# An attention kernel whose instruction order moves from hand-woven streams to a list scheduler

## The chip, the core and the metric

The kernel runs on one core of a Trainium2 chip. A core has five engines that run side by side, each on its own queue of instructions: TensorE (PE, matmuls and transposes into the PSUM banks), VectorE (DVE), ScalarE (ACT), GpSimd (POOL) and SyncE (SP, which here issues nearly all DMAs). [...] The metric is the device time of one execution in microseconds (us).

## The reference

Inputs are `x` (2 batches of 2048 rows, 640 wide) and a context of 128 tokens (384 wide) per batch, of which 124 are text and the last 4 feed an adapter. All is float32, 8 heads of 80. Cut to what matters:

```python
query = x @ Wq
hs = mha(query, text @ Wk, text @ Wv)              # text attention: 2048 queries, 124 keys
ca_q1 = einsum('btc,th->bch', ca, Wq_ca)           # (384, 640) from the 4 tokens
ca_q1 = ca_q1[:, indices]                          # 2048 rows, only 384 different ones
ca_hs1 = mha(ca_q1, x, x)                          # 384 queries over 2048 rows of x
ca_hs2 = mha(ca_hs1 @ Wq, ca @ Wk_ca, ca @ Wv_ca)  # over the 4 tokens
out = (hs + ca_hs2) @ Wout + b_out + x
```

So two things are computed for each batch: text attention, which is most of the work, and the adapter, a long chain whose result is a table `o2` of 384 rows that is added to the output rows by index.

## The kernel before

*Adapter.* `x` comes in blocks of 512 rows (4 per batch). `x_load` (L766) issues eight DMAs per block into one staging tile `xi`, and `x_turn` (L785) makes five 32-by-32 block transposes on VectorE into `xt`. `yz_block` (L800) multiplies a block by small prepared weights (`pyz`) and makes two operands, `yz` and `zop` (ScalarE copy, VectorE shuffle `zs`, ScalarE cast, VectorE subtraction). `maxima` (L843) goes over a batch in 24 steps: four matmuls (`s1`) fill one tile of four PSUM banks, VectorE takes the maximum of 2048 columns (`mx`). There is one such tile, so a step's matmuls wait for the maximum of the step before. `less_maxima` (L862) turns the maxima into an operand `cop`. `contraction` (L882) has 32 steps: four matmuls (`s2`) into the same tile, an exponential on ScalarE (`ea`), four matmuls that add it up with `y_sb` (`acc`). A short chain then gives `p2`, and `o2` is written to memory.

*Text.* `queries` (L991) makes the 25 matmuls `pq` of a block. A unit `m` is two tiles of 128 rows, 16 units in all. `scores` (L1026): ten matmuls `sc` per tile into two banks, maxima `m` and differences `p` on VectorE, exponential on ScalarE. `divided` (L1065): sums and reciprocals `r` on VectorE, product on POOL. `turned_out` and `turned` (L1089, L1075): a block transpose `eb`, written to memory as `kept` and read back as `pT`, which completes the transposition. `values` (L1114): 16 matmuls `ph`, copied out as `hsT`, then 20 output matmuls `po`, each half tile added on VectorE to the rows `xo` of `x` that `residual` (L1099) has loaded. If `o2` is already in memory, its rows are added by an indirect DMA on POOL (`add_second`, L1165) and the rows go out; otherwise they go to memory as `early`, and `completed` (L1173) fetches and finishes them later.

*What sets the order.* TensorE's instructions and SP's DMAs are pinned to program order. On VectorE a few instructions have order dependencies by hand (`VectorBehind`, L49); the rest of VectorE, ScalarE and POOL is ordered by the framework. Program order is woven from streams: `weave` (L1229) draws one step of the adapter, and then a `Mix` (L136) of `Fill`s (`own`, `text`, `later`) is run for as many microseconds of TensorE time as that step's gap says; TensorE's time is counted in `TensorInOrder` (L21). A fill is a fixed sequence of parts, and it stops at a part whose conditions are not met. `rows_stages` (L1284) holds the conditions of a block: its five transposes may come only when 18 or 24 us of TensorE work have passed since the load:

```python
stage(
    (("again" if again else "x") if k == 4 else ("turned", k), b, sb), x_turn(k),
    lambda k=k: Mix.hurry or pe.us > coming[0] + after + 0.6 * k,
)
```

PSUM has eight banks: four for the adapter's tile, three that text and the rest turn over in order (`mm_tile`, L263), and one that `acc` and some others use. When the adapter is done, its four go to text.

Of the kernel before, what the change touches and what calls it, by code (L numbers as in the profile page):

```python
# [14 lines left out]
P = 128  # L15
HEADS = 8
T = 4
WITHIN = "within"


class TensorInOrder:  # L21

    def __init__(self, tc):
        self.tc, self.us = tc, 0.0

    def matmul(self, out, lhsT, rhs, **kw):
        ins = self.tc.nc.tensor.matmul(out, lhsT, rhs, **kw)  # L29
        self.tc.keep_in_program_order(ins)  # L30
        n = 1
        for size in rhs.shape[1:]:
            n *= size
        if lhsT.dtype == F32R:
            self.us += (n / 2.4 + 215) / 4e3
        elif min(lhsT.shape[0], lhsT.shape[1]) <= 32:
            self.us += (n / 1.2 + 97) / 2e3
        elif min(lhsT.shape[0], lhsT.shape[1]) <= 64:
            self.us += (n / 1.2 + 54) / 1e3
        else:  # L40
            self.us += 2 * max(n / 1.2, 109) / 1e3

    def transpose(self, out, in_, ident):
        ins = self.tc.nc.tensor.transpose(out, in_, ident)
        self.tc.keep_in_program_order(ins)
        self.us += 0.109


class VectorBehind:  # L49

    def __init__(self, tc):
        self.tc, self.last, self.bound = tc, None, None

    def __getattr__(self, name):
        def call(*args, **kw):
            self.last = getattr(self.tc.nc.vector, name)(*args, **kw).ins  # L58
            if self.bound is not None:
                self.behind(self.last, self.bound)  # L60
            return self.last

        return call

    def behind(self, ins, other):
        kind = mybir.DependencyInfo(mybir.DependencyClass.NoSync, mybir.DependencyReason.DATA)
        self.tc.add_manual_dep(ins, other.name, kind, reason="order on VectorE")

    def close(self):
        self.bound = self.last  # L70


class Fill:


    def __init__(self, done, *parts):
        self.done, self.parts, self.open, self.us = done, list(parts), False, 0.0

    def add(self, *parts):
        self.parts += parts  # L80

    def blocked(self):

        return not self.parts or any(
            not w() if callable(w) else w not in self.done
            for w in getattr(self.parts[0], "needs", ())
        )

    def step(self, pe):

        if self.blocked():
            return False
        before = pe.us
        at = next(self.parts[0], self)
        self.us += pe.us - before
        self.open = at is WITHIN
        if at is self:
            self.parts.pop(0)
        return True


class Stage:


    def __init__(self, done, what, gen, *needs):
        self.done, self.what, self.gen, self.needs = done, what, gen, needs

    def __iter__(self):
        return self

    def __next__(self):
        self.needs = ()
        try:
            return next(self.gen)
        except StopIteration:
            self.done.add(self.what)
            raise


class Slots:  # L120


    def __init__(self, done, pool, number):
        self.done, self.pool = done, pool
        self.users = [set() for _ in range(number)]

    def free(self, n):
        return lambda: sum(u <= self.done for u in self.users) >= n

    def tile(self, shape, name, users):  # L130
        at = next(i for i, u in enumerate(self.users) if u <= self.done)
        self.users[at] = set(users)
        return self.pool.tile(shape, F32, tag=f"slot{at}", name=name)


class Mix:  # L136

    hurry = False  # L140

    def __init__(self, pe, *fills):
        self.pe, self.fills, self.at = pe, [[f, w, f.us] for f, w in fills], None

    def step(self):
        if self.at is not None and self.at.open:
            return self.at.step(self.pe)
        for f, w, us in sorted(self.fills, key=lambda x: (x[0].us - x[2]) / x[1]):
            if f.step(self.pe):
                self.at = f  # L150
                return True
        return False

    def run(self, us=None):

        while us is None or us > 0:
            before = self.pe.us
            if not self.step():
                return 0.0
            if us is not None:  # L160
                us -= self.pe.us - before
        return us

    def until(self, done, what):
        while what not in done:
            for f, _, _ in self.fills:
                if any(getattr(p, "what", None) == what for p in f.parts):
                    while self.at is not None and self.at is not f and self.at.open:
                        self.at.step(self.pe)
                    self.at = f  # L170
                    if not f.step(self.pe) and what not in done and not self.step():
                        Mix.hurry = True
                        assert f.step(self.pe), what
                        Mix.hurry = False
                    break
            else:
                assert what in done, what
# [3 lines left out]
def kernel(  # L181
# [14 lines left out]

    nc = tc.nc
    pe = TensorInOrder(tc)
    dve = VectorBehind(tc)
# [17 lines left out]
    MAX = 4 * T  # L241


    const = ctx.enter_context(tc.tile_pool(name="const", bufs=1))
    xrow = ctx.enter_context(tc.tile_pool(name="xrow", bufs=4))
    xqp = ctx.enter_context(tc.tile_pool(name="xqp", bufs=1))
    hbm = ctx.enter_context(tc.tile_pool(name="hbm", bufs=2, space=bass.MemoryType.DRAM))
    done = set()
    slots = Slots(done, xqp, NSB + 1)
    ps_m = ctx.enter_context(tc.tile_pool(name="ps_m", bufs=3, space=bass.MemoryType.PSUM))  # L250
    ps_a = ctx.enter_context(tc.tile_pool(name="ps_a", bufs=1, space=bass.MemoryType.PSUM))

    def dma(out, in_):

        tc.keep_in_program_order(nc.sync.dma_start(out, in_))

    matmul = pe.matmul
    transpose = pe.transpose

    ps_turns = [ps_m]  # L260
    ps_turn = [0]

    def mm_tile(name, pool=None):  # L263
        if pool is None:
            pool = ps_turns[ps_turn[0] % len(ps_turns)]
            ps_turn[0] += 1
        return pool.tile([P, 512], F32, tag="mm", name=name)

    on = ["A"]
    turn = [0]  # L270

    def evacuate(dst, src):

        turn[0] += 1
        if on[0][turn[0] % len(on[0])] == "A":
            nc.scalar.copy(dst, src)  # L276
        else:
            dve.tensor_copy(dst, src)

# [4 lines left out]
    def band(t, pattern, width, base=0):  # L284

        nc.gpsimd.memset(t, 1.0)
        nc.gpsimd.affine_select(
            out=t, in_=t, compare_op=ALU.is_ge, fill=0.0,
            base=base, pattern=pattern, channel_multiplier=1,
        )  # L290
        nc.gpsimd.affine_select(
            out=t, in_=t, compare_op=ALU.is_ge, fill=0.0,
            base=width - 1 - base, pattern=[[-a, n] for a, n in pattern], channel_multiplier=-1,
        )
# [6 lines left out]

# [5 lines left out]
    dve.tensor_reduce(ones, ones4, AX.X, ALU.add)  # L307

    VH = 2 * R
    VR = D - VH  # L310
# [9 lines left out]

# [3 lines left out]


# [11 lines left out]
    N2 = 3 * G + 2 * B * T  # L337
    w2_sb = const.tile([N2 + 1, H], F32, name="w2_sb")
    p2pad = const.tile([P, NCC, P], F32, name="p2pad")


    cap = ctx.enter_context(tc.tile_pool(name="cap", bufs=1))
    small = ctx.enter_context(tc.tile_pool(name="small", bufs=3))
# [3 lines left out]


    ctx_sb = sp.tile([NTOK, B, CAD], F32, name="ctx_sb")
    dma(ctx_sb, enc.rearrange("b t c -> t b c"))  # L350
    wqca_sb = sp.tile([T, H], F32, name="wqca_sb")
    dma(wqca_sb, Wq_ca)

    def by_chunk(t):

        g = t.rearrange("p (c d) -> p c d", c=4)
        return g[:, :, :P], g[:, :, P:]

    def load_x(b, st, name):
        t = xrow.tile([P, H], F32, tag="x", name=f"{name}_{b}_{st}")  # L360
        dma(t, x[b, st * P : (st + 1) * P, :])
        return t

    def block_rows(name):

        return xrow.tile([P, 4 * H], F32, tag="xz", name=name, bufs=1)
# [7 lines left out]
    for name, bands in (  # L374
# [4 lines left out]
        for n, (pattern, width, base, factor) in enumerate(bands):  # L379
            m = const.tile([P] + [k for _, k in pattern], F32, name=f"band_{name}_{n}")  # L380
            band(m, pattern, width, base)
            if n == 0:
                dve.tensor_reduce(low[name], m, AX.XY if len(pattern) == 2 else AX.X, ALU.add)
            else:
                r = const.tile([P, 1], F32, name=f"sum_{name}")
                dve.tensor_reduce(r, m, AX.X, ALU.add)
                dve.scalar_tensor_tensor(low[name], r, factor, low[name], ALU.mult, ALU.add)

    def halves_of(to, whole, name):

        nc.scalar.copy(to, whole)
        dve.scalar_tensor_tensor(to, to, low[name], whole, ALU.mult, ALU.subtract)
# [1016 lines left out]
```

## Time and profile before

| | us |
|---|---|
| runs | 737.92, 738.15, 747.12 (median 738.15) |
| the profiled execution's own time | 740.3 |
| its span, first to last instruction | 738.6 |
| TensorE busy in it | 663.3 |

The profile is that of one execution. Busy time is the time in which an engine executes; a wait is put down to whatever released the engine last. Groups of instructions go by the names of the tiles they write and read; where a helper issues an operation, the line is the helper's (L29 is the helper of all matmuls, L58 that of VectorE's operations, L255 that of SP's DMAs). Both score stages of the adapter appear as `s`, the maxima as `s<-zop,cop`, the contraction as `s<-cop,zop`. A float32 matmul of the program stands as two passes in most groups. Rows in order of time give the start, the length, the engine, the instruction with its count, and in brackets the idle time before it with what ended it. The trace's clock is the share of full speed granted to TensorE.

### The profile page before, as it was taken

To read this page: it belongs to the slowest core of one execution; us is meant where nothing else is said; L and a number is where in the kernel's file an instruction comes from. 1 tells how busy PE (TensorE), PEld (TensorE's weight loads), DVE (VectorE), ACT (ScalarE), POOL (GpSimd) and SP (SyncE) were. 2 spreads that over 40 slices of the span, in tenths; PEclk is the share of its full clock that TensorE was granted. 3 is DMA by queue.
4 is the path that set the end of the run, shared out by engine and by line. 5 is a ranking of instruction groups with operands and counts; after the bars stand their busy time and mean duration, and the time that the engine had idled before them with its cause. 6 is when DMAs were issued, how large, how long until landed. Compare 5 with 4: busy or idle time off the path is not lost.

```text
span 738.6 us, 9123 instructions
## 1 busy us (share of the span) xinstructions
PE 663.3 (90%) x3611; PEld 339.1 (46%) x3611; DVE 395.9 (54%) x565; ACT 206.9 (28%) x264; POOL 142.3 (19%) x213
## 2 busy tenths in 40 slices
PE   7967999979899988889999527999999999999997
PEld 4533443334344434454545213344444655555664
DVE  2247837765547175566798767126035546246631
ACT  2321222215545441222121104545443111011100
POOL 8200000015210111211344001102001143132320
PEclk9997999989999999799999757999999999999999
DMA  8808140002954684498499605704139378456882
GB/s 293 179 1 138 23 71 1 0 1 69 166 161 71 187 149 126 134 174 258 75 270 235 141 0 119 138 19 142 27 116 141 102 208 232 131 133 175 223 238 81
DMA packets 147363, 95.04 MB, mean 129 GB/s; under 512 B 118517, under 2 KB 119413, under 8 KB 145274
## 3 DMA queue, kind: packets, MB, share of 16 engines
q1 hardware_dynamic: 141690, 83.79, 45.7%
q0 software_dynamic: 5632, 10.69, 8.3%
q8 instruction: 28, 0.46, 0.3%
q14 instruction: 13, 0.11, 0.1%
HBM read 63.26 MB, written 31.20 MB: 128 GB/s over the span
## 4 chain that ended last, share of the span: by engine, by line
PE 72%; DVE 20%; issue 3%; ACT 2%; DMA 2%; POOL 0%; SPq 0%; DVEq 0%; ACTq 0%; POOLq 0%
PE po L29 22%; PE pq L29 21%; DVE mx L58 6%; PE sc L29 6%; PE acc L29 5%; PE s L29 5%; PE ph L29 4%; PE pyz L29 3%; DVE p L58 3%; DVE m L58 3%; DVE eb L58 3%; DVE xt L58 3%; DMA pT<-kept 1%; PE pk L29 1%; PE pv L29 1%
## 5 line engine op out<-in xcount | busy, mean ns | idle before, releaser
L29 PE MATMUL po<-wout_sb,hsT 128*128 128x320 f32 x640 | 187.0, 439 | 1.8 <-DVE hsT L58 1.3
L29 PE MATMUL pq<-xt,wq_sb 128*128 128x512 f32 x320 | 152.4, 607 | 0.0
L29 PEld LDWEIGHTS po<-wout_sb,hsT 128*128 128x128 f32 x640 | 118.3, 190 | 72.8 <-issue 24.0
L58 DVE TENSOR_REDUCE mx<-s 128x4 f32<-128x2048 f32 x48 | 109.7, 2284 | 23.3 <-PE s L29 23.3
L913 ACT ACTIVATE ea<-s 128x1536 f32<-128x1536 f32 x64 | 92.8, 1450 | 89.9 <-PE s L29 89.7
L58 DVE TENSOR_TENSOR xo<-xo,po 128x320 f32<-128x320 f32 x64 | 30.9, 484 | 160.1 <-PE po L29 160.1
L29 PEld LDWEIGHTS pq<-xt,wq_sb 128*128 128x128 f32 x320 | 56.9, 190 | 66.3 <-issue 61.8
L1072 POOL TENSOR_TENSOR p<-p,r 128x992 f32<-128x992 f32 x32 | 61.4, 1989 | 97.5 <-DVE r L58 89.0
L1057 ACT ACTIVATE p<-p 128x992 f32<-128x992 f32 x32 | 33.0, 1030 | 107.2 <-DVE p L58 106.9
L1167 POOL DMA_INDIRECT xo<-o,query x26 | 40.6, 1560 | 116.1 <-DMA xo<-in_x_dram 51.4
L29 PE MATMUL sc<-kmain,q 64*128 64x124 f32 x512 | 44.4, 300 | 17.2 <-DVE p L58 17.0
L58 DVE TENSOR_REDUCE m<-sc 128x4 f32<-128x496 f32 x64 | 41.8, 662 | 33.2 <-PE sc L29 33.2
L29 PE MATMUL s<-zop,cop 32*128 32x512 f32 x192 | 27.3, 556 | 32.5 <-DVE mx L58 25.5
L29 PE MATMUL acc<-ea,y_sb 128*32 128x384 f32 x512 | 55.6, 507 | 0.0
L29 PEld LDWEIGHTS sc<-kmain,q 64*128 64x128 f32 x512 | 37.4, 201 | 36.0 <-issue 24.5
L276 ACT COPY q<-pq 128x512 f32<-128x512 f32 x31 | 18.1, 585 | 120.9 <-PE pq L29 120.7
L29 PE MATMUL ph<-pT,vpad 128*32 128x256 f32 (+1 forms) x512 | 50.6, 392 | 1.2 <-DMA pT<-kept 1.2
L1058 POOL MEMSET p<- 128x32 f32 x32 | 6.2, 216 | 211.0 <-DVE eb L58 211.0
L58 DVE TENSOR_TENSOR p<-sc,m 128x496 f32<-128x496 f32 x64 | 42.1, 668 | 1.4
L58 DVE STREAM_TRANSPOSE eb<-p 128x1024 f32<-128x1024 f32 x32 | 38.1, 1222 | 5.9 <-POOL p L1072 5.9
L29 PEld LDWEIGHTS s<-zop,cop 32*128 32x128 f32 x192 | 10.2, 203 | 62.7 <-DVE mx L58 43.7
L29 PEld LDWEIGHTS ph<-pT,vpad 128*32 128x32 f32 (+1 forms) x512 | 23.9, 125 | 31.7 <-issue 12.9
(167 smaller groups left out, 549.6 us busy)
## 6 DMA issues: line engine op xcount, KB each, us to landing
kept<-eb SPq DMA_DIRECT2D x16, 1024.0 KB, 5.1
pT<-kept SPq DMA_DIRECT2D x64, 256.0 KB, 5.8
xi<-in_x_dram SPq DMA_DIRECT2D x44, 256.0 KB, 4.8
xo<-in_x_dram SPq DMA_DIRECT2D x32, 320.0 KB, 5.4
out_dram<-xo SPq DMA_DIRECT2D x24, 320.0 KB, 3.5
xi<-in_x_dram SPq DMA_DIRECT2D x44, 64.0 KB, 4.7
early<-xo SPq DMA_DIRECT2D x6, 320.0 KB, 2.2
o<-o SPq DMA_DIRECT2D x6, 320.0 KB, 2.2
```

What stands on the lines that cost most here:

```text
L29: ins = self.tc.nc.tensor.matmul(out, lhsT, rhs, **kw)
L58: self.last = getattr(self.tc.nc.vector, name)(*args, **kw).ins
L276: nc.scalar.copy(dst, src)
L913: nc.scalar.activation(e, q4[:, :, :CAD], AF.Exp, scale=SCALE)
L1057: nc.scalar.activation(e[:, :, :NK], e[:, :, :NK], AF.Exp, scale=SCALE)
L1058: nc.gpsimd.memset(e[:, :, NK:], 0.0)
L1072: nc.gpsimd.tensor_tensor(et, et, r.unsqueeze(2).to_broadcast([P, HEADS, NK]), ALU.mult)
L1167: nc.gpsimd.indirect_dma_start(out=t, out_offset=None, in_=o2_of[b], in_offset=bass.IndirectOffsetOnAxis(ap=query[:, st : st + 1], axis=0) ...
```

## The change

The streams, gaps and conditions go, with the classes TensorInOrder, VectorBehind, Fill, Stage, Slots and Mix. In their place every piece of work is a task, a generator that yields operations (`Do`): engine or engines, function, what it waits for, which buffers it needs (`Room`s, counted and numbered), what it frees, a rank. A `Desk` holds a clock of its own. It takes the operation that can start first, over all engines, and among those of an engine that can start at once the one of lowest rank; it calls its function, which issues the instructions and adds their estimated times, and sets the times at which its results and buffers come free. Every instruction on all five engines is pinned in the order so found. A copy out of PSUM that ScalarE or VectorE can do goes to the one that is free first.

The adapter has rank 0, text unit `m` 30 + m (scores 1.7 less, residual 0.5 less), and the first finishing steps of a unit rank 1. Adapter work of batch 1 may begin before batch 0's contraction ends. PSUM's four banks outside the adapter's tile are one `Room`; a score tile needs two free ones to begin. The transposes of a block follow when its load is reckoned to have landed. Early output tiles are fetched, added to and written one at a time (`xp`). The four padding columns of the probabilities are cleared once per buffer instead of once per tile, and the last unit's output rows leave whole instead of in halves. Matmuls and operands are the same.

```diff
-class TensorInOrder: ...
-class VectorBehind: ...
-class Fill: ...
-class Stage: ...
-class Slots: ...
-class Mix: ...
+class Room:
+    def __init__(self, n):
+        self.at = [0.0] * n
...
+class Desk:
+    ENGINES = ("PE", "ACT", "DVE", "POOL", "SP", "NONE")
+    TAIL = {"PE": 0.25, "DVE": 0.18, "ACT": 0.2, "POOL": 0.25, "SP": 0.1, "NONE": 0.0}
...
+    def run(self):
+        while any(self.queue.values()):
+            best = None
+            for e in self.ENGINES:
+                found = [(max(r, self.free[e], self.now), op) for op in self.queue[e] if (r := self.ready(op)) is not None]
+                if found:
+                    t = min(x[0] for x in found)
+                    op = min((x[1] for x in found if x[0] <= t + 1e-9), key=lambda x: x.order)
+                    if best is None or t < best[0]:
+                        best = t, e, op
...
+            self.issue(*best)
+
+    def issue(self, t, engine, op):
...
+        op.slots = [room.take(n) for room, n in op.needs]
+        op.value = op.fn(*op.slots)
+        self.free[engine] = t + self.spent if engine != "NONE" else 0.0
+        end = t + self.spent + self.TAIL[engine] if self.landed is None else self.landed
...
+    def matmul(self, out, lhsT, rhs, **kw):
+        self.pin(self.nc.tensor.matmul(out, lhsT, rhs, **kw))
...
+        self.spent += (1 if one else 2) * max(n / 2.4 * (1 if one else 2), 109) / 1e3 / at_once
...
+        base, each = {"v": (0.06, 1.04), "a": (0.13, 0.77), "g": (0.1, 2.0)}[side]
...
+    def dma(self, out, in_, us, issue=0.45):
+        self.pin(self.nc.sync.dma_start(out, in_))
+        self.spent += issue
+        self.channel = max(self.channel, self.now + self.spent) + us
+        self.landed = self.channel + 1.9
...
+    banks, slots, rows, staging = Room(4), Room(NSB + 1), Room(4), Room(1)
...
+    def x_load(b, sb, again, after):
...
+        for i in range(4):
+            part = slice(R * i, R * (i + 1))
+            yield Do("SP", lambda: dma(most[part], v[:, :, :, R * i : R * (i + 1)], 2.2, 1.3), [])
+            op = yield Do("SP", lambda: dma(rest[part], v[:, i, :, P:], 0.6, 0.6), [])
+        landed = op.at
...
+            yield Do(
+                "DVE", turn, [landed], frees=[(staging, 0)] if k == 4 else [],
+                marks=[(kind, b, sb)] if k == 4 else [], rank=3,
+            )
...
+    def adapter(b):
...
+                    op = yield Do("PE", scores, [("zop", b, sb, u), c_at], needs=[(quad, 1)])
+                    op = yield Do(
+                        "DVE",
+                        lambda q4=op.value: desk.v_tensor_reduce(mx[:, ct, u, :, sb], q4, AX.X, ALU.max),
+                        frees=[(quad, 0)], rank=5,
+                    )
...
+        if b + 1 < B:
+            yield Fork(adapter(b + 1), 0)
...
+    def text_scores(m):
...
+            op = yield Do(
+                "PE", product, [("q", n), "keys", "late"], needs=[(banks, 2), (es, 1)], marks=[("sc", m, k)],
+            )
+            yield Fork(softmax(m, k, op.value, op.slots[0], op.slots[1][0], op.at), 30 + m - 1.7)
...
+    def added(m, k, u, po, s, at):
...
+        if early[m] and not desk.known(("o2", b)):
+            part = hbm.tile([P, H], F32, tag=f"early_{m}_{k}", name=f"early_{b}_{st}")
+            op = yield Do("SP", lambda: dma(part, t, 1.3), both, frees=[(rows, i)])
+            yield Do("NONE", lambda: None, [op.at, ("o2", b)])
...
+            op = yield Do("SP", load, needs=[(rows, 1), (ending, 1)], rank=-1)
...
-    for sb in range(NSB):
-        fill.until(done, ("yzT", 0, sb))
-        fill.run(yz_at[0, sb] + 5.0 - pe.us)
-        weave(maxima(0, sq, mx_of[0], sb, 2.3), fill, 2.0)
...
-    weave(contraction(0, sq, 2.0), fill, 0.8)
...
+    begin(adapter(0), 0)
+    for m in range(UNITS):
+        begin(text(m), 30 + m)
+    desk.run()
```

More of the change, by code (lines that the diff above doesn't have):

```diff
@@ L49 @@
[L49 to L70, printed above, removed]
@@ L73 @@
[L73 to L99, printed above, removed]
@@ L102 @@
[L102 to L133, printed above, removed]
@@ L136 @@
[L136 to L177, printed above, removed]
@@ L248 @@
[L248 to L267, printed above, removed]
@@ L481, in spread_yz, with by_groups @@
                 )
[L483 to L487 removed]
+    def by_groups(at, name, rows_, w):
+        pg = bank(at, name)
         for cc in range(NCC):
@@ L659, in load_wout, with count @@
+        yield Do("POOL", steps_of, ["keys"])
+        def count():
+            desk.v_tensor_reduce(counted, steps, AX.X, ALU.add)
+            desk.v_tensor_tensor(counted, counted, first, ALU.add)
+            desk.v_tensor_copy(query, counted)
+        yield Do("DVE", count, marks=["query"])
     def load_wout():
@@ L1366 @@
[L1366 to L1379 removed]
+        ))
```

1841 lines of the change are left out of this document (1044 added, 797 removed).

## The prediction

> **What bounds the kernel now.** I read the page first, then the busy time of each engine in seven stretches cut at TensorE's marks (first score of each adapter stage, last matmul), then the list of waits, then single stretches in order of time. The page:
>
> ```profile
> span 738.6 us, 9123 instructions
> PE 663.3 (90%) x3611; PEld 339.1 (46%) x3611; DVE 395.9 (54%) x565; ACT 206.9 (28%) x264; POOL 142.3 (19%) x213
> PE   7967999979899988889999527999999999999997
> PEclk9997999989999999799999757999999999999999
> ```
>
> TensorE is busy for 663.3 of 738.6 us, and no other engine comes near that. So a new order, which leaves the matmuls what they are, can at most take the 75.3 us in which TensorE is idle, plus what it lost at a lower clock. The stretches say where the 75.3 are (length, then busy time and instruction count by engine, then granted clock, DMA share, GB/s):
>
> ```profile
> 0.00:52.70 52.70, 43.71 (x225) 25.47 (x225) 13.52 (x56) 15.22 (x32) 19.61 (x96) 1.00 0.59 166
> 52.70:165.90 113.20, 99.00 (x403) 43.52 (x403) 78.80 (x75) 24.43 (x51) 2.49 (x7) 0.94 0.24 38
> 165.90:324.50 158.60, 146.15 (x955) 72.31 (x955) 83.21 (x136) 68.41 (x67) 32.28 (x39) 0.94 0.59 136
> 324.50:407.10 82.60, 77.04 (x375) 38.74 (x374) 65.72 (x72) 16.89 (x28) 28.55 (x22) 0.98 0.91 204
> 407.10:446.90 39.80, 15.53 (x71) 6.68 (x70) 29.04 (x24) 4.50 (x7) 0.00 (x0) 0.60 0.30 62
> 446.90:554.00 107.10, 103.91 (x685) 46.08 (x685) 38.84 (x62) 52.28 (x43) 11.19 (x12) 0.97 0.39 97
> 554.00:735.50 181.50, 177.94 (x914) 106.34 (x906) 86.81 (x144) 25.17 (x38) 48.17 (x38) 1.00 0.66 168
> ```
>
> Idle TensorE, row by row: setup 9.0; maxima of batch 0 14.2; contraction of batch 0 and what follows it 12.5; maxima of batch 1 5.6 and then 24.3; contraction of batch 1 3.2; the text tail 3.6; and 3.1 after the last matmul. A third of it is one hole, from 407 to 447. The list of waits names what TensorE waited for (total, times, longest), and two rows in order of time show the hole from inside:
>
> ```profile
> PE s L29 <- DVE mx L58: 25.5, 14, 3.3
> PE sc L29 <- DVE p L58: 17.0, 9, 5.9
> PE s L29 <- DVE zop L58: 7.0, 2, 3.7
> 435.28 0.80 PE L29 MATMUL s<-zop,cop 32*128 32x512 f32 x4 [2.40 <-DVE mx L58]
> 438.48 0.80 PE L29 MATMUL s<-zop,cop 32*128 32x512 f32 x4 [2.40 <-DVE mx L58]
> ```
>
> In the hole the adapter runs alone: four matmuls, a maximum on VectorE, four matmuls, 3.20 us a step, 2.40 of it idle. The fill streams have nothing left that their conditions allow. The clock of that stretch is 0.60, and the four matmuls take 0.80 where they take 0.51 at full clock (below).
>
> **The change part by part.**
>
> *The same matmuls.* Both built kernels issue 2110 matmuls with the same operands (the trace shows most of them as two passes). I counted the other engines in the same way: 30 memsets on POOL go (POOL is 19% busy: nothing), 12 copies move from VectorE to ScalarE (28% busy: nothing). So the floor stays near 663, and the question is the idle time.
>
> *The hole.* A filled step before, and the adapter's pyz at full clock and in the hole:
>
> ```profile
> 69.94 3.00 PE L29 MATMUL pyz<-xt,wyz 128*64 128x512 f32 x12
> 85.25 0.51 PE L29 MATMUL s<-zop,cop 32*128 32x512 f32 x4
> 85.69 2.84 PE L29 MATMUL pq<-xt,wq_sb 128*128 128x512 f32 x6
> 88.46 0.51 PE L29 MATMUL s<-zop,cop 32*128 32x512 f32 x4
> 410.48 4.64 PE L29 MATMUL pyz<-xt,wyz 128*64 128x512 f32 x12
> ```
>
> Six passes of queries between two scores give a step of 3.21 us and no wait. In the built order of the changed kernel none of the 48 maxima steps holds less: the thinnest have these six passes, or their worth in text matmuls; six of batch 1's steps lie inside batch 0's contraction, and the usual step holds 4 to 5 us. In the order before, the last ten steps hold no text matmul. What fills them comes out of the tail: after the last adapter score the order before holds 166 output and 50 query matmuls, the new one 101 and 25. So 24.3 us of idle goes, less 3 that I leave for steps whose filler is itself late; and the lost clock comes back, seven lone scores at 0.29 and the pyz at 1.64, 3.7. **-25.**
>
> *Banks.* The 17.0 us of sc waiting for p are score tiles whose bank VectorE had not yet emptied: TensorE starts a tile and stands in it. The new kernel begins a tile only when two of four banks are free by its own clock, and does something else otherwise. I take half of that idle. **-8** (-17 to 0).
>
> *Setup.* The 7.0 us on zop are the first two scores. In the new order 2 query and 6 key matmuls stand ahead of the first and 18 small ones ahead of the second.
>
> ```profile
> 9.21 0.66 PE L44 MATMUL pt_x<-ident,xz 128*128 128x128 f32 x4 [0.64 <-DMA xz<-in_x_dram]
> ```
>
> VectorE's first copies now stand behind the band sums. That costs nothing as long as x's rows, which land at 9, are later. **-4** (-7 to 0).
>
> *More changes of shape.* Adapter and text matmuls alternate more. In the filled step the six passes begin at 85.69 and end 2.77 later with the next score; in the tail (next rows) an output unit takes 11.03 for 40 passes of 320 columns, so that six of 512 take 2.6. A change costs about 0.16, and I count 31 more. **+5.**
>
> *The end.* Last rows before:
>
> ```profile
> 689.04 1.05 PE L29 MATMUL sc<-kmain,q 64*128 64x124 f32 x16
> 689.93 1.00 PE L29 MATMUL sc<-krest,q 64*128 64x496 f32 x4
> 704.97 0.34 SPq L255 DMA_DIRECT2D kept<-eb  x1
> 711.46 1.75 SPq L255 DMA_DIRECT2D pT<-kept  x4
> 721.04 2.95 PE L29 MATMUL ph<-pT,vpad 128*64 128x256 f32 x32 [1.24 <-DMA pT<-kept]
> 723.91 11.03 PE L29 MATMUL po<-wout_sb,hsT 128*128 128x320 f32 x40
> ```
>
> From the last scores to the ph that reads their probabilities pass 30.1 us (690.9 to 721.0): 14 in softmax, 6.5 to memory, 9.6 back. TensorE covers them with two units, 2 x (2.95 + 11.03) = 28. In the new order only one unit, 14.0 us, lies between the last scores and the last ph. The softmax is that of one tile instead of two, shorter by about 5 (rows below: two m, two p, r, eb make 5.0), so 25 are needed and 11 are idle where 1.2 were. The last tile also leaves in one piece of 640 columns instead of two halves, 1 more. **+11** (+6 to +16).
>
> *VectorE.* The new order moves eight tiles of softmax into the maxima of batch 0.
>
> ```profile
> L58 DVE TENSOR_REDUCE mx<-s 128x4 f32<-128x2048 f32 x48 | 109.7, 2284 | 23.3 <-PE s L29 23.3
> L58 DVE TENSOR_TENSOR p<-sc,m 128x496 f32<-128x496 f32 x64 | 42.1, 668 | 1.4
> L58 DVE TENSOR_REDUCE m<-sc 128x4 f32<-128x496 f32 x64 | 41.8, 662 | 33.2 <-PE sc L29 33.2
> L58 DVE STREAM_TRANSPOSE eb<-p 128x1024 f32<-128x1024 f32 x32 | 38.1, 1222 | 5.9 <-POOL p L1072 5.9
> L58 DVE TENSOR_REDUCE r<-p 128x8 f32<-128x992 f32 x32 | 37.1, 1160 | 0.0
> L58 DVE STREAM_TRANSPOSE xt<-xi 128x512 f32<-128x512 f32 x55 | 34.5, 680 | 0.0
> ```
>
> 24 maxima (54.8), 16 pairs of m and p (21.3), 8 eb (9.8), 8 r (9.3), 15 block transposes (10.2) and an estimated 19 of zs, zop and small ones: 124 us. TensorE has 99.0 in that stage before; now 12 query matmuls fewer (-10), seven score tiles at 1.9 (+13), two units and a third ph more (+29): 131. Two engines this full with a chain between them wait for each other. The densest stretch before, 324 to 407, has VectorE at 80% and TensorE 5.6 us idle in 82.6; that rate would give 9. With VectorE fuller I take 14, as much as the stage has now. **0** (-5 to +12).
>
> *Loads and the queue that issues them.* Everything on SP is in one written order, before and after. Before, the transposes of a block are held back by 18 or 24 us of TensorE work after its load (the condition in rows_stages). Now they stand where the load is reckoned to have landed: transfers of 11.2 us behind the first issue of 1.3, and 1.9 more, about 14. The trace has eleven loads, here the shortest and the longest (start, length of the eight issues), and issue to landing:
>
> ```profile
> 57.99 8.33 SPq L255 DMA_DIRECT2D xi<-in_x_dram  x8
> 394.66 17.68 SPq L255 DMA_DIRECT2D xi<-in_x_dram  x8
> DMA to landing us min/median/max: 3.7/4.8/14.0
> ```
>
> 8.3 + 4.8 = 13 when little else moves, 17.7 + 4.8 = 22.5 beside other transfers. So VectorE, in order, will stand in front of a late block for 0 to 8 us, and kept, pT and the output rows behind it on SP are late with it. Nothing late: 0. With a mean of 4 on eleven loads, all of it reaching TensorE: 44. TensorE has a bank or two of other work at such a place, so I take a fifth, nearer to the short row. **+8.**
>
> *Early tiles.* 21 output tiles instead of 6 go to memory and back before the adapter's part is added, since text now runs ahead of the adapter: 15 more writes and 15 more reads of 320 KB.
>
> ```profile
> early<-xo SPq DMA_DIRECT2D x6, 320.0 KB, 2.2
> xe<-early SPq DMA_DIRECT2D x6, 320.0 KB, 5.4
> ```
>
> No matmul reads them, so I cost them at nothing. If that cover goes, their issue (a third of a microsecond each by the kept row, 10 in all) lies in front of pT. [...]
>
> *Sum.* -25 - 8 - 4 + 5 + 11 + 0 + 8 = -13: a span of about 726. The profiled execution took 740.3, 1.7 above its span, and the median of the runs is 738.15; on the median's scale the forecast is 738.2 - 13 = **725 us**, faster by 1.8%. Two per cent, 14.8 us, is about what a measurement of this kernel can tell from no change: below 723.4 counts as faster, above 752.9 as slower.
>
> **The rivals.**
>
> *The plan holds.* By its constants the new kernel reckons 2.19 us for the maximum and 1.13 for eb, close to the rows. So the loads may be hidden, VectorE no hindrance and all waits on banks gone: -25 - 17 - 4 + 5 + 9 - 5 + 0 = -37, **701 us**. For it: in the stretch 446 to 554, as finely mixed as the new order, TensorE idles 3.2 in 107. Against it: there VectorE is at 36%.
>
> *The one that ends slower: the block loads.* VectorE and SP each take the next instruction in order, so a late block stops the maxima, the banks and the probabilities behind it. If three quarters of the 44 us reach TensorE, no bank wait is saved beyond 4, and VectorE and the end cost their upper ends: -25 - 4 - 4 + 5 + 16 + 12 + 33 = +33, **771 us**. It decides from the point where each of the eleven loads leaves more than 1.3 us idle on TensorE with those upper ends (then the sum passes 752.9), or more than 3.3 with the terms as I took them. For it: 17.7 of issue against a reckoned 14 to landing, and the 24 us held back are gone. Against it: the usual maxima step holds 1 to 2 us more matmuls than the 3.2 of its chain, so a lag is made up over a few steps. [...]
>
> *The order is not what runs.* Where something moved instructions after all, the hole would stay: about 738. The built order shows the pins honoured on all five queues, so this gets almost nothing.
>
> **How the numbers follow.** Forecast (715 to 745) 0.50; the plan holds (690 to 715) 0.27; slower by late loads (745 to 785) 0.21; no effect 0.02. Faster by over 2%: all of the second and a third of the first, 0.27 + 0.17 = 0.44. Slower: 0.17 of the third's 0.21. Within 2%: the rest, 0.39. Range for 8 in 10: 698 to 760.
>
> **What would show it.** Right: no stretch of lone scores; idle before sc below 9 us; some 10 us of idle before the last ph, behind DMA pT. Late loads would show as idle of xt behind DMA xi, a wait that VectorE does not have now, and as s waiting for mx with xt in front. Wrong would be: TensorE idle well above 14 in the maxima of batch 0, or its busy time above 675 (then the changes of shape were mis-sized).

## The result and the profile after

The kernel after takes 685.4 us in the median (685.24 to 685.51, four runs); the kernel before took 741.6 beside it (737.92 to 747.12). The ratio is 0.924, with a 95% interval of 0.916 to 0.931: 7.6% faster. The forecast was 725 with a range of 698 to 760, so the time lies 13 us below the lower end. It lies below even the rival called "the plan holds" (701).

The page of the profiled execution after (span, TensorE's row, its busy tenths and the granted clock in 40 slices):

```profile
span 683.7 us, 9125 instructions
PE 645.5 (94%) x3611; PEld 329.9 (48%) x3611; DVE 389.7 (57%) x553; ACT 214.6 (31%) x276; POOL 139.7 (20%) x183
PE   6999999999999999999899999999999999996097
PEclk9999999999999999999899999999999999999589
```

Of the 54.9 us that the span lost, 37.1 are idle TensorE (75.3 before, 38.2 now). The other 17.8 are busy time, 663.3 to 645.5, with the same 3611 passes. The row of tenths has one gap left, near the end. The busy time by stretch (length, then busy time and count by engine, granted clock, DMA share, GB/s), cut at the same marks as before, with the tail in three:

```profile
0.00:48.20 48.20, 41.97 (x220) 24.45 (x220) 19.07 (x66) 11.23 (x22) 19.43 (x94) 1.00 0.94 230
48.20:178.24 130.04, 129.30 (x674) 65.76 (x673) 119.81 (x141) 32.45 (x60) 17.99 (x16) 1.00 0.48 112
178.24:334.39 156.15, 151.53 (x983) 73.20 (x981) 84.26 (x123) 70.54 (x73) 21.53 (x23) 0.98 0.54 116
334.39:441.88 107.49, 107.29 (x492) 54.31 (x491) 85.57 (x94) 24.31 (x41) 19.07 (x12) 1.00 0.73 165
441.88:555.90 114.02, 114.02 (x755) 52.39 (x754) 37.71 (x58) 57.67 (x51) 22.48 (x15) 1.00 0.56 145
555.90:627.10 71.20, 71.17 (x355) 40.78 (x352) 33.07 (x56) 14.32 (x24) 26.08 (x16) 1.00 0.80 215
627.10:649.72 22.62, 0.02 (x3) 0.03 (x1) 6.37 (x8) 1.03 (x1) 11.53 (x7) 0.58 1.07 286
649.72:680.42 30.70, 30.17 (x144) 18.99 (x144) 3.90 (x8) 3.08 (x6) 1.55 (x1) 0.92 0.48 153
```

From 48 to 627 us TensorE idles 5.6 us. The maxima of batch 0 (second row) are the surprise: 0.7 idle in 130 us with VectorE at 92%. The list of waits, TensorE's and then VectorE's row for the block loads (total, times, longest):

```profile
PE ph L158 <- DMA pT<-kept: 22.6, 1, 22.6
PE s L158 <- DVE mx L179: 0.5, 2, 0.3
PE sc L158 <- DVE p L179: 0.4, 1, 0.4
...
DVE xt L179 <- DMA xi<-in_x_dram: 0.2, 1, 0.2
```

The waits on mx (25.5 before) and on p (17.0) are gone, and VectorE stands behind a late block for 0.2 us in all. What is left, beside some 6 us in the setup, is one wait of 22.6 on the probabilities of the last unit but one.

The fallen busy time sits mostly in the score tiles. The groups by form, before:

```profile
L29 PE MATMUL sc<-kmain,q 64*128 64x124 f32 x512 | 44.4, 300 | 17.2 <-DVE p L58 17.0
L29 PE MATMUL sc<-krest,q 64*128 64x496 f32 x128 | 38.3, 638 | 0.0
```

and after:

```profile
L158 PE MATMUL sc<-kmain,q 64*128 64x124 f32 x512 | 37.6, 284 | 0.4 <-DVE p L179 0.4
L158 PE MATMUL sc<-krest,q 64*128 64x496 f32 x128 | 32.7, 579 | 0.0
```

The two rows add up to 82.7 before and 70.3 now, but matmuls of the two groups overlap: as time of TensorE the score tiles fell from 73.9 to 64.1, 9.8 of the 17.8. The adapter's scores `s` fell by 4.2 more (57.1 to 52.9). Two tiles of before, in order of time, show why; the first was not held up, the second was:

```profile
290.06 1.16 PE L29 MATMUL sc<-kmain,q 64*128 64x124 f32 x16
291.05 1.00 PE L29 MATMUL sc<-krest,q 64*128 64x496 f32 x4
...
299.01 2.41 PE L29 MATMUL sc<-kmain,q 64*128 64x124 f32 x15 [5.94 <-DVE p L58]
...
301.42 1.86 PE L29 MATMUL sc<-krest,q 64*128 64x496 f32 x3
```

After standing 5.94 us for a bank, the tile runs at about half speed, with a granted clock of 0.50 where the first tile has 1.00: 4.3 us from 299.01 to its end instead of 2.0. So this wait on a bank cost its 5.94 us of idle and then 2.3 in a slow stretch behind it, which the page counts as busy.

### The profile page after: what moved, and what is told of

Read it like the earlier page. It is cut to its first block, busy times and chain, and to the rows that moved or that the text cites. A ratio compares the mean times of both kernels' runs of the same rounds, so it can differ in the third digit from the quotient of the medians.

```text
span 683.7 us, 9125 instructions
## 1 busy us (share of the span) xinstructions
PE 645.5 (94%) x3611; PEld 329.9 (48%) x3611; DVE 389.7 (57%) x553; ACT 214.6 (31%) x276; POOL 139.7 (20%) x183
## 2 busy tenths in 40 slices
DMA packets 151395, 104.87 MB, mean 153 GB/s; under 512 B 118965, under 2 KB 119349, under 8 KB 149306
## 4 chain that ended last, share of the span: by engine, by line
PE 84%; DVE 8%; DMA 5%; POOL 1%; issue 1%; SPq 0%; ACT 0%; DVEq 0%; ACTq 0%; POOLq 0%
PE po L158 26%; PE pq L158 24%; PE acc L158 7%; PE sc L158 7%; PE s L158 6%; PE ph L158 6%; PE pyz L158 3%; DVE mx L179 2%; DMA pT<-kept 2%; DMA xo<-o,query 1%; DVE p L179 1%; DVE m L179 1%; DMA xp<-early 1%; DMA xp<-o,query 1%; PE pv L158 1%; PE pk L158 1%
## 5 line engine op out<-in xcount | busy, mean ns | idle before, releaser
L158 PE MATMUL po<-wout_sb,hsT 128*128 128x320 f32 x640 | 183.8, 439 | 0.0
L158 PE MATMUL ph<-pT,vpad 128*32 128x256 f32 (+1 forms) x512 | 53.3, 409 | 23.4 <-DMA pT<-kept 22.6
L179 ACT ACTIVATE p<-p 128x992 f32<-128x992 f32 (+1 forms) x34 | 33.5, 987 | 90.9 <-DVE p L179 90.9
L1478 POOL DMA_INDIRECT xp<-o,query x21 | 32.8, 1561 | 121.7 <-DMA xp<-early 70.3
L158 PEld LDWEIGHTS ph<-pT,vpad 128*32 128x32 f32 (+1 forms) x512 | 24.5, 128 | 53.6 <-issue 38.2
L179 ACT COPY q<-pq 128x512 f32<-128x512 f32 x36 | 21.0, 584 | 85.8 <-PE pq L158 85.8
L179 ACT COPY hsT<-ph 128x512 f32<-128x512 f32 (+1 forms) x44 | 22.5, 517 | 69.5 <-PE ph L158 69.4
L179 DVE TENSOR_REDUCE r<-p 128x8 f32<-128x992 f32 (+1 forms) x34 | 38.0, 1117 | 9.3 <-ACT p L179 9.1
L158 PEld LDWEIGHTS sc<-kmain,q 64*128 64x128 f32 x512 | 31.8, 187 | 14.7 <-issue 7.4
L158 PE MATMUL sc<-kmain,q 64*128 64x124 f32 x512 | 37.6, 284 | 0.4 <-DVE p L179 0.4
L158 PE MATMUL pq<-xt,wq 128*128 128x512 f32 x80 | 37.9, 604 | 0.0
```

What stands on the lines that cost most here:

```text
L158: self.pin(self.nc.tensor.matmul(out, lhsT, rhs, **kw))
L179: self.pin(getattr(engine, what)(*args, **kw))
L1478: desk.pin(nc.gpsimd.indirect_dma_start(out=t, out_offset=None, in_=o2_of[b], in_offset=bass.IndirectOffsetOnAxis(ap=query[:, st : st + 1] ...
```

## The experiments

Times in each group are from one chip, beside the kernel before. The kernel after, run again with the tails below, took 685.9 (685.38 to 687.15; ratio to before 0.924, 0.918 to 0.930). The kernels between the first experiment and the three tails were timed once each, so differences of one or two us among them say nothing.

**The hole alone.** In the kernel before, one number of the written order:

```diff
-        weave(maxima(1, sq, mx_of[1], sb, 4.8), fill, 2.0)
+        weave(maxima(1, sq, mx_of[1], sb, 4.0), fill, 2.0)
```

> The kernel before with one number changed: in the maxima of batch 1 the fill between two scores is asked for 4.0 us instead of 4.8. In its built order none of the 24 steps of these maxima is left without text or query matmuls (before, ten of the last ten had none but the adapter's own). Theory A, the hole is worth what it looked like and no scheduler is needed for it: 24 us of idle and 4 of clock go, busy falls from 663 to about 658, the time from 741.6 to about 714. Theory B, the filler is only moved: it is missing later, the idle comes back in the contraction of batch 1 or in the tail, 730 or more. Theory C, the hole also cost clock around it: below 708, with a busy time under 653.

Measured: 731.4 us in the median of four runs against 744.5, ratio 0.980 (0.976 to 0.984). Its waits:

```profile
PE sc L29 <- DVE p L58: 24.4, 8, 7.9
PE s L29 <- DVE mx L58: 11.2, 8, 3.6
```

The wait on mx fell by 14.3, but the wait on p rose by 7.4, and busy rose to 668.1. With filler in every step the score tiles come into the full stretch, and there VectorE cannot follow. This is nearest to theory B, though the idle comes back on p and not in the places that it named. In the old order the filler is worth about 13 us, and the other 43 come from something that this ration does not give.

**Whose order?** The kernel after, with `keep_in_program_order` left out for some engines: first for VectorE, ScalarE and POOL together (the diff), then for each of the three alone. TensorE's 2110 matmuls stand in the same order in all four.

```diff
     def pin(self, ins):
-        self.tc.keep_in_program_order(ins)
+        if self.engine in ("PE", "SP"):
+            self.tc.keep_in_program_order(ins)
```

> The kernel after with the order kept on TensorE and SP alone; the other engines' instructions are placed as without the scheduler (539 on VectorE, of which 397 keep their place in the sequence, 258 of 278 on ScalarE, 148 of 185 on POOL). TensorE's and the queue's order are the same. Theory A, TensorE's order carries the gain, the others only follow: 683 to 692. Theory B, VectorE is 92% busy in the maxima of batch 0 and its order is part of the plan, so that scores wait for maxima behind work that is not urgent: 700 to 730, with idle on mx and p.

> The kernel after with VectorE's order free (404 of its 539 instructions keep their place in the sequence), the other four engines as planned. Theory A, it is VectorE's order that the full stages need: 730 to 765, idle on mx, xt and behind p. Theory B, it is POOL's products, and VectorE only follows: below 705.

> The kernel after with POOL's order free (151 of 185 keep their place), the others as planned. Theory A (VectorE's order decides): 685 to 695. Theory B (POOL's products late behind the additions, eb waits for p, 60.7 us when all three were free): 720 to 765.

> The kernel after with ScalarE's order free (266 of 278 keep their place), the others as planned. Both theories: 684 to 692; above 700 would mean that copies out of a bank placed late hold up TensorE.

| order free on | us | TensorE busy / idle |
|---|---|---|
| VectorE, ScalarE and POOL | 767.2 | 669.1 / 96.4 |
| VectorE | 745.6 | 661.6 / 82.3 |
| POOL | 685.5 | 644.3 / 39.5 |
| ScalarE | 692.1 | 646.8 / 43.6 |

With VectorE's order free, the whole gain is gone: 745.6 against 743.9 of before. TensorE runs the new order there. Of the 60 us, 44 are idle and 16 are busy time, nearly the 17.8 by which the busy time had fallen. While the other two stay planned, POOL's order is worth nothing and ScalarE's about 7 us. All three free cost 22 more than VectorE's alone, beyond the range of that run's theory B, so the orders do not simply add up. The run with VectorE free again waits for late maxima, in the first row. The other rows show one place of it, TensorE's row first and then VectorE's in order of time:

```profile
PE s L159 <- DVE mx L180: 15.3, 11, 2.6
...
463.73 1.82 PE L159 MATMUL sc<-kmain,q 64*128 64x124 f32 x13 [7.88 <-DVE p L180]
...
453.42 1.25 DVE L180 TENSOR_REDUCE m<-sc 128x4 f32<-128x496 f32 x2
455.49 2.29 DVE L180 TENSOR_REDUCE mx<-s 128x4 f32<-128x2048 f32 x1 [0.82 <-PE s L159]
457.70 3.07 DVE L180 STREAM_TRANSPOSE xt<-xi 128x512 f32<-128x512 f32 x5
460.70 2.33 DVE L180 STREAM_TRANSPOSE eb<-p 128x1024 f32<-128x1024 f32 x2
462.95 1.22 DVE L180 TENSOR_TENSOR p<-sc,m 128x496 f32<-128x496 f32 x2
```

Between a tile's m and the p that frees its banks VectorE does a maximum, five block transposes and two eb, 7.7 us. The kernel before does the like ahead of its wait of 5.94:

```profile
294.28 1.21 DVE L58 TENSOR_REDUCE m<-sc 128x4 f32<-128x496 f32 x2
...
295.94 2.36 DVE L58 STREAM_TRANSPOSE eb<-p 128x1024 f32<-128x1024 f32 x2
298.23 1.21 DVE L58 TENSOR_TENSOR p<-sc,m 128x496 f32<-128x496 f32 x2
```

The scheduler's order, in the kernel after:

```profile
97.14 0.67 DVE L179 TENSOR_REDUCE m<-sc 128x4 f32<-128x496 f32 x1
97.84 0.67 DVE L179 TENSOR_TENSOR p<-sc,m 128x496 f32<-128x496 f32 x1
...
99.76 0.62 DVE L179 TENSOR_REDUCE m<-sc 128x4 f32<-128x496 f32 x1
100.42 0.68 DVE L179 TENSOR_TENSOR p<-sc,m 128x496 f32<-128x496 f32 x1
```

Each m has its p behind it, because both are one task (`less` in `softmax`) that is issued at once; eb comes later. VectorE's total work is 390 us in either case. What differs is which piece a bank or a score waits for. The other half, the old order of TensorE with a better one on VectorE, was not tried.

**Do the plan's numbers matter?** VectorE reckoned at 0.6 of its durations:

```diff
-        base, each = {"v": (0.06, 1.04), ...
+        base, each = {"v": (0.036, 0.62), ...
```

> The kernel after, planned with VectorE's operations at 0.6 of their durations (2.19 for the maximum becomes 1.31); the work is the same. Theory A, the saved bank and maxima waits hang on the plan's durations: in the maxima of batch 0, where VectorE is at 92%, TensorE starts scores that VectorE cannot take, sc waits for p and s for mx again, 20 to 35 us of idle and some 5 to 10 of clock: 705 to 730. Theory B, a fixed order of about the right kind is enough, and VectorE's backlog is made up: below 692.

Measured: 730.0. The row that grew:

```profile
PE s L158 <- DVE mx L179: 23.9, 25, 2.2
```

Theory A, at its upper end and with one correction: the idle is on the maxima, not on the banks of score tiles. A planner that believes a maximum takes 1.3 us puts its next score after too little filler, 25 times. Busy is 659.1.

**Banks.** Only the two banks of a score tile reckoned free too soon:

```diff
             yield Do("DVE", less, ..., frees=[(banks, s[u])], rank=1)
+            banks.at[s[u]] -= 3.0
```

> The kernel after, where the plan alone takes the two banks of a score tile to be free 3 us before VectorE has emptied them; durations and work are the same. Theory A, a wait on a bank is what the new order saved, and it costs more than its idle: TensorE stands in front of sc, pq, po or ph behind p for 15 to 30 us in all, and what follows a wait runs at a lower clock, busy 650 or more: 700 to 720. Theory B, my sum's view, about half of what waits there would have been idle anyway: 688 to 697. Theory C, the bank is never the last thing waited for: below 688.

Measured: 691.9, which is theory B. TensorE stands 6.7 us behind p in all (in front of po 2.7, sc 2.1, ph 1.0, pyz 0.9). While VectorE's own order stays sensible, a bank reckoned free 3 us too soon costs little.

**Loads.** In two ways, the plan taking them to land too soon. First, every block of x by 9 us:

```diff
         landed = op.at
+        landed.t -= 9.0
```

> The kernel after, where the plan takes each block of x to have landed 9 us sooner than before, so that its block transposes stand sooner in VectorE's order. Theory A, the loads are hidden because the plan has them wait for one shared channel, and TensorE has a bank or two of other work: VectorE stands 11 times in front of a late block, 30 to 60 us in all, of which a fifth reaches TensorE: 690 to 698. Theory B, my rival of late loads, three quarters reach TensorE: 710 to 730. Theory C, the loads have so much room that 9 us cost nothing: 683 to 688 and less than 10 us of VectorE behind xi.

Second, every DMA without the channel that they share in the plan:

```diff
-        self.channel = max(self.channel, self.now + self.spent) + us
-        self.landed = self.channel + 1.9
+        self.landed = self.now + self.spent + us + 1.9
```

> The kernel after, where the plan reckons each DMA for itself (issue, its own transfer, 1.9 us) and not in turn behind all the others on one channel. A block of x is then reckoned to land about 10 us after its first issue instead of 14 and more. Theory A, the shared channel in the plan is why no load was late: VectorE stands in front of xi for 20 us or more in all, and pT and kept are late too: 692 to 710. Theory B, the channel makes no difference, the loads are hidden anyway: 680 to 688.

The first took 700.0, the second 723.2. What VectorE stood behind, in the first:

```profile
DVE xt L179 <- DMA xi<-in_x_dram: 23.6, 4, 8.4
```

and in the second:

```profile
DVE xt L179 <- DMA xi<-in_x_dram: 31.2, 5, 10.6
DVE xt L179 <- DMA wout_sb<-in_L_xattn_Wout_dram: 8.9, 1, 8.9
```

Nine microseconds too soon cost 14 us (between theories A and B), with four late blocks instead of eleven. A plan in which every transfer has the DMA engines to itself costs 38 us and is beyond theory A. VectorE stands 31.2 us behind blocks and once more 8.9 in front of xt, which the profile puts down to a weight's load; TensorE stands behind pT for 21.8, no longer than in the kernel after (22.6). Since VectorE's time behind late blocks rises from 0.2 us to 31.2, the shared channel in `Desk.dma` is what keeps the loads hidden.

**Overlap.** The adapter of batch 1 begun only after the contraction of batch 0:

```diff
-        if b + 1 < B:
-            yield Fork(adapter(b + 1), 0)
         for j in range(2):
...
         yield Fork(second(b), 0)
+        if b + 1 < B:
+            yield Fork(adapter(b + 1), 0)
```

> The kernel after, where the adapter of batch 1 may begin only after the last contraction score of batch 0 (before, six steps of its maxima lie inside that contraction). Theory A, the overlap carries part of the gain, since the maxima of batch 1 run short of filler without it: a stretch of lone scores comes back, idle on mx 8 to 15 us, 695 to 710. Theory B, the plan rations the filler with or without it, no lone scores, and only the tail shifts: 683 to 693.

Measured: 688.6, waits on mx 0.5 as in the kernel after. Theory B: the overlap carries about 3 us.

**The tail.** First, the second part of twelve tiles of batch 1 left out:

```diff
-        early[m] = not desk.known(("o2", b))
-        if early[m]:
+        early[m] = b == 0 and not desk.known(("o2", b))
+        if early[m] or not desk.known(("o2", b)):
```

> The kernel after, where twelve output tiles of batch 1 go out without the adapter's part (left out: eight trips to memory and back and twelve indirect additions), so that SP and POOL are freer behind TensorE's last 80 us; TensorE's work is the same. Theory A, the idle before the last but one ph (22.6 us) is there because pT stands on SP behind stores that wait for POOL's additions: it falls below 9 and the time to 666 to 674. Theory B, my sum's view, the chain softmax, memory and back is too long for the one unit beside it, whatever the queue does: 11 or more remain, 676 to 684.

Measured: 671.9. TensorE's rows of its tail:

```profile
631.02 4.79 PE L158 MATMUL ph<-pT,vpad 128*64 128x256 f32 x32 [5.13 <-DVE r L179]
...
650.87 4.50 PE L158 MATMUL ph<-pT,vpad 128*64 128x256 f32 x32 [4.08 <-DMA pT<-kept]
```

The 22.6 became 5.1 and 4.1. The time is theory A's; the 9.2 that remain are just over its bound and below that of theory B. About 9 are the chain that I had reckoned at 11, and the other 13.5, which is the whole gain in time, come with the second part. How can be read in the kernel after, here TensorE's hole, the queue's issues and two additions on POOL:

```profile
649.72 5.37 PE L158 MATMUL ph<-pT,vpad 128*64 128x256 f32 x32 [22.60 <-DMA pT<-kept]
...
621.74 1.45 SPq L199 DMA_DIRECT2D kept<-eb  x1
633.16 0.34 SPq L199 DMA_DIRECT2D out_dram<-xp  x1
635.65 0.34 SPq L199 DMA_DIRECT2D out_dram<-xo  x1
636.09 3.10 SPq L199 DMA_DIRECT2D pT<-kept  x4
...
623.54 1.55 POOL L1478 DMA_INDIRECT xp<-o,query  x1 [3.28 <-issue]
625.40 1.54 POOL L1478 DMA_INDIRECT xo<-o,query  x1 [0.30 <-issue]
```

pT leaves 0.1 us after the second store, which had to wait for its addition. From an addition's start to its store pass 9.6 and 10.2 us; the plan has 1.6 + 6.0. In the run without these additions pT follows kept after 6.0 us:

```profile
617.20 0.33 SPq L199 DMA_DIRECT2D kept<-eb  x1
...
623.25 1.75 SPq L199 DMA_DIRECT2D pT<-kept  x4
```

Here it took 14.3, so SP held it for about 8, if kept landed as fast here as there. Then 13.6 us pass from pT's issue to ph, where the last unit of that run needs 8.4 (642.47 to 650.87). Those 5 I put down to DMA traffic, of which the share here is 1.07; no run takes the traffic away alone.

Then three tails with the second part in place, timed together. The first:

```diff
-        desk.landed = desk.now + desk.spent + 6.0
+        desk.landed = desk.now + desk.spent + 9.5
...
-            op = yield Do("POOL", lambda: add_second(t, b, st), [*both, ("o2", b), "query"])
+            op = yield Do("POOL", lambda: add_second(t, b, st), [*both, ("o2", b), "query"], rank=80)
...
-        yield Fork(text_scores(m), 30 + m - 1.7)
+        yield Fork(text_scores(m), 30 + m - 2.7)
```

`softmax` has the same 2.7, and the products on POOL have rank 0. The second has 3.2 in these two places and beside that:

```diff
-                ending.at += [desk.now] * 3
+                ending.at += [desk.now] * 2
...
-        yield Do("SP", lambda: dma(rows_out, t, 1.3), both, frees=[(rows, i)] + own)
+        yield Do("SP", lambda: dma(rows_out, t, 1.3), both, frees=[(rows, i)] + own, rank=80)
...
-        begin(queries(n, [("x" if b == 0 else "again", b, sb)]), 30 + 2 * n - 2.5)
+        begin(queries(n, [("x" if b == 0 else "again", b, sb)]), 30 + 2 * n - 6.5)
```

The third has `* 1` there, and kept and pT are tasks of ScalarE, which issues their DMAs.

> The kernel after, unchanged, on the chip of the three tails below. Both theories: 684 to 687, with 22 to 23 us of idle before the last but one ph.

> The kernel after with four numbers of the plan changed: an indirect addition is reckoned to land 9.5 us after its issue instead of 6.0 (the trace has 9.6 to 11 from its start to the store behind it), the additions of early tiles come last and the products of probabilities first on POOL, and scores rank a unit further ahead (2.7 instead of 1.7). Theory A, the hole is SP standing in front of pT behind stores whose additions the plan takes to land too soon: it falls below 10, the time to 671 to 677. Theory B, DMA traffic itself is the limit there (share 1.07), so that any order gives the same: 681 to 688.

> As the run before, but at most three early tiles on their way back at once instead of four, their stores last on SP, scores 3.2 and queries 6.5 ahead of their unit instead of 1.7 and 2.5. Theory A, the last tiles' scores come earlier, so that two units stand beside their chain and the idle in the tail is 5 or less: 666 to 674. Theory B, text run this far ahead takes filler from the maxima: lone scores come back, 680 or more.

> As the run before, with kept and pT issued by ScalarE instead of SP and at most two early tiles on their way back. Theory A, the stores that wait for additions no longer stand in front of pT, no idle in the tail, but the early tiles finish later, behind the last matmul: 668 to 676. Theory B, ScalarE stands in front of kept and pT and its evacuations are late, in the contraction above all: 690 or more.

| | us | ratio to before (95%) |
|---|---|---|
| after | 685.9 | 0.924 (0.918 to 0.930) |
| additions reckoned longer | 676.0 | 0.911 (0.905 to 0.916) |
| scores and queries earlier, fewer early tiles | 673.5 | 0.908 (0.902 to 0.914) |
| the same, pT on ScalarE's queue | 675.9 | 0.911 (0.905 to 0.916) |

All three beat both kernels. The best (672.62 to 674.62) lies 12.4 below the kernel after, with no overlap of their times. Its row for the tail:

```profile
PE ph L158 <- DMA pT<-kept: 8.2, 2, 7.3
```

All three times lie in the range of their theory A, but more idle is left than each theory allowed. The first tail has 10.4 there, just over its 10; since four numbers changed in it at once, it does not show what the longer addition alone is worth. The second has 8.2 for its 5, and no lone scores. ScalarE's queue leaves 4.3, and the time is no better: TensorE's idle in all is the same as in the second (26.9 and 26.5) and its busy time 2.7 longer.

## Why the prediction was wrong

| term | forecast | measured |
|---|---|---|
| hole, with the maxima of batch 1 | -25 | -29.6 idle (29.8 to 0.2), of it 4.1 on p |
| banks and VectorE (maxima and contraction of batch 0) | -8 and 0 | -21.3 idle (26.7 to 5.4); sc of the whole kernel -9.8 busy |
| contraction of batch 1 | none | -3.2 idle |
| setup | -4 | -2.8 idle; of the 7.0 on zop, all gone, 3.7 lie in the row of batch 0 |
| changes of shape | +5 | none visible |
| loads | +8 | 0.2 on VectorE |
| the end | +11 | +19.8 idle |
| early tiles | 0 | in the end's row |

The idle rows add up to -37.1 and the busy time fell by 17.8, together the 54.9 by which the span fell. The forecast had -14 of idle and, with the changes of shape and the lost clock of the hole, +1 of busy time. So of the 42 us that it missed, 23 are idle and 19 are busy time.

**Hole: right.** No step is thin, and no lone score is left. The size was right, too. But the first experiment shows that the fill alone, in the old order, brings 13: its score tiles need VectorE as well.

**VectorE: the step that failed.** "The densest stretch before ... that rate would give 9. With VectorE fuller I take 14." This carried a rate of idle per VectorE load from the old order to the new one, as if the load made the waits. That stage now idles 0.7 us, with VectorE at 92%. The order of VectorE's queue makes the waits: at the same 390 us of work TensorE idles 38 with the planned order and 82 without it, and is busy 645.5 and 661.6. In the diff, this change of VectorE's queue stands as plainly as TensorE's; I had compared TensorE's steps only. With VectorE's order free one score tile stood 7.88 us for a p that came behind xt and eb. I had used the order of VectorE's queue for a rival that ends slower, and it is as much the reason for the gain.

**Banks: half was wrong twice.** Nearly all of the 17.0 went, and "half of that idle" priced a wait at its idle alone. The tile behind the wait of 5.94 us ran at about half speed (granted clock 0.50), and sc lost another 9.8 of busy time. For lost clock I had counted only the hole, 3.7.

**Loads: wrong.** "About 14" took the plan's landing time as a constant. In `Desk.dma` it is the end of a channel that all SP's transfers share, so that a busy queue moves the reckoned landing by itself. With that undone the kernel takes 723, the direction in which the rival of late loads pointed, though not slower than before. My "fifth" looks too low as well: in the run with 23.6 us of VectorE behind blocks the time rose by 14, if the changed plan moved nothing else. The trips of early tiles added bytes (95.04 MB became 104.87) and stretched nothing that TensorE waited for between 48 and 627 us. In the hole (DMA share 1.07) traffic, with the additions, may cost the 5 us above; that is my estimate, and no run shows it apart.

**Changes of shape: wrong or hidden.** Busy time fell, and outside the tail only small groups of matmuls got longer (most of all `po<-w_sb,p2T`, by 1.7 us, and `pv`, by 0.6); an upper bound is not to be had from these runs.

**The end: right in kind, too small.** The idle stands behind DMA pT as forecast, but one unit earlier, before the last ph but one. The chain was 9 for the 11 forecast. The other 13.5 belong to "No matmul reads them, so I cost them at nothing": the text itself gave the price if that cover went, 10 us of issue in front of pT. It was not the issue but, for about 8, the wait for POOL's additions in front of it; the rest stays open.

**The rivals.** "The plan holds" had the right mechanism, with 0.27; it took only 5 off the maxima of batch 0 and left the clock out.

## What to carry to other kernels

Where a busy second engine empties the first one's buffers, compare that engine's order between the two kernels as closely as the first one's: here it was worth 60 us at unchanged work, under the new order of TensorE. Price a wait on TensorE that is not short (here, for score tiles, from 2.26 us, with 1.77 instead of 1.00 for the three passes behind it) as its idle plus the slow matmuls behind it, and look for the second half in the busy time of the same group. In a queue with one written order, an instruction that waits for something reckoned too short (here an addition of 10 us reckoned at 7.6) holds what stands behind it (here pT, for an estimated 8 us), and a planner is only as good as its longest latencies.

## What the runs showed of the hardware beside that

Score tiles of before that waited 2.26 us or more ran slower, and one that waited 1.83 did not, as two of them show:

```profile
331.89 1.01 PE L29 MATMUL sc<-kmain,q 64*128 64x124 f32 x13 [2.26 <-DVE p L58]
332.85 1.77 PE L29 MATMUL sc<-krest,q 64*128 64x496 f32 x3
...
375.80 1.01 PE L29 MATMUL sc<-kmain,q 64*128 64x124 f32 x13 [1.83 <-DVE p L58]
376.76 1.00 PE L29 MATMUL sc<-krest,q 64*128 64x496 f32 x3
```

Behind 2.26 us of idle the three long passes take 1.77 instead of 1.00; behind 1.83 us they do not. The other score tiles that waited 1 us or more agree: in the 2 us behind a wait of 2.26, 2.28, 2.45 and 5.94 us the granted clock is 0.76, 0.87, 0.63 and 0.50, behind 1.10 and 1.83 us it is 1.00. What a wait between 1.83 and 2.26 us costs was not tried.
